# Attention result kept by tokens in a two-layer convolution/attention kernel with a chunked recurrence: transposes moved from ScalarE copies and an early pass to TensorE at the end

## The chip, the cores and the metric

The kernel runs on one core of a Trainium2 chip. A core has five engines with their own instruction streams: TensorE (PE, matrix products; it loads weights, written PEld in the profile, and streams columns through them into PSUM), VectorE (DVE), ScalarE (ACT), GpSimd (POOL) and SyncE (SP, here the issuer of nearly all transfers). SBUF is the working memory of 128 partitions, PSUM the small memory that PE writes and DVE and ACT read. Transfers between SBUF and the external memory (HBM) run on DMA engines.

The metric is the device time of one execution in microseconds; lower is better. All numbers are float32.

## What is computed

The input x has shape (4, 128, 64, 64): 4 batches, 128 channels, N = 4096 positions, which the second layer calls tokens.

```python
def reference(x, wq, wk, wv, wo, Wq, Wk, Wv, W, V, gamma, beta):
    # layer 0: attention over positions, 64-wide q, k, v; no mask
    q, k, v = (einsum('mc,bcn->bmn', w, xf) for w in (wq, wk, wv))
    att = softmax(einsum('bmi,bmj->bij', k, q), axis=2)
    x = x + einsum('cm,bmn->bcn', wo, einsum('bij,bmj->bmi', att, v))
    # layer 1, by tokens: t is (b, n, c)
    t = x.transpose to (b, n, c)
    t = t + causal_attention(layernorm(t), Wq, Wk, Wv)      # scale 128 ** -0.5
    wx = batchnorm(layernorm(t) @ W.T) * gamma + beta       # mean, var over b and n
    y[i] = sigmoid(wx[i] + y[i-1] @ V.T)                    # recurrence over the tokens
    t = t + y
    return t.transpose back to (b, c, h, w)
```

## The kernel before

B = 4 batches, P = 128, N = 4096, BLK = 512 tokens to a block, NB = 8 blocks, TPB = 4 tiles of 128 tokens to a block.

**Attention.** Both layers run over a list of items (pairs of 128 keys for a block of 512 queries). For each item PE computes scores (line 649 in layer 0, 658 in layer 1), ACT the exponential, DVE the sums, and PE the weighted values (709 and 717), two items later. What is to be done after the last item of a block is spread over the next items as a chain of steps. In layer 1 the chain is this; each `yield` gives the number of items to wait:

```python
def transposed(src, dst, name, engine):
    ps = misc(name)                         # one PSUM bank, two of them in turn
    for j in range(TPB):
        nc.tensor.transpose(ps[:, ts(j, P)], src[:, j], ident)
    engine(dst, ps)

def finish1(b, g):
    def first():
        project(1, b, g, agg, den)          # xs[:, b, block] += attention, by tokens
        mem["xh"] = wk.tile([P, TPB, P], F32, tag="xh2", name="xh2")
        normed(b, g, mem["xh"])             # layernorm by tokens
    def second():
        t = xs[:, b, ts(g, BLK)].rearrange("p (j c) -> p j c", c=P)
        xc = wk.tile([P, BLK], F32, tag="xc", name="xc")
        transposed(t, xc, "tT_ps", nc.scalar.copy)
        nc.sync.dma_start(out=x2[b, :, ts(g, BLK)], in_=xc)
        mem["xhT"] = wk.tile([P, BLK], F32, tag="xhT2", name="xhT2")
        transposed(mem["xh"], mem["xhT"], "xh2T_ps", nc.vector.tensor_copy)
    def third():
        wp = misc("wx_ps")
        nc.tensor.matmul(wp, lhsT=wf, rhs=mem["xhT"], start=True, stop=True)
        ...
        nc.vector.bn_stats(stats[:, b * NB + g], wp)
        nc.scalar.copy(                     # wx overwrites the tokens in xs, sorted by step
            xs[:, b, ts(g, BLK)].rearrange("p (s c) -> p s c", c=CPB),
            wp.rearrange("p (c s) -> p s c", s=STEPS))
    yield 1, first
    yield 3, second
    yield 1, third
```

The tokens after attention are needed again at the end, so they are put aside in HBM (`x2`), here turned to channels by tokens.

**Recurrence.** It is cut into NCH = 256 chunks of STEPS = 16 tokens, which run side by side as 256 columns; each chunk is warmed up with the 12 tokens before it. In all 28 rounds of 4 batches, each of a matmul, an addition by DVE and a sigmoid by ACT:

```python
with ... tc.tile_pool(name="ps_y", bufs=2, space=PSUM) as ps_y:
    xr = xrp.tile([P, B, N], F32, name="xr")
    for b in range(B):
        nc.sync.dma_start(out=xr[:, b], in_=x2[b])
    ...
    by_step = xs.rearrange("p b (g s c) -> p b s g c", s=STEPS, c=CPB)
    def step(b, s):
        wx = by_step[:, b, s % STEPS]
        ...                                 # y: where the state goes; for s >= 0 it replaces wx
        ps = grid(ps_y.tile([P, NCH], F32, tag=f"y{b}", name="y_ps"))
        nc.tensor.matmul(ps, lhsT=vf, rhs=prev[b], start=True, stop=True)
        z = grid(yp.tile([P, NCH], F32, tag=f"z{b}", name="z"))
        nc.vector.scalar_tensor_tensor(z, in0=wx, scalar=scale, in1=ps, op0=ALU.mult, op1=ALU.add)
        nc.scalar.activation(y, z, AF.Sigmoid, bias=shift)
```

**Residual.** At the end ACT sorts the states back to token order and DVE adds them to the loaded tokens:

```python
def residual(b):
    for h in range(2):
        for g in range(h * NB // 2, (h + 1) * NB // 2):
            y = yp.tile([P, BLK], F32, tag="yt", name="yt")
            nc.scalar.copy(y.rearrange("p (c s) -> p c s", s=STEPS),
                           xs[:, b, ts(g, BLK)].rearrange("p (s c) -> p c s", c=CPB))
            t = xr[:, b, ts(g, BLK)]
            nc.vector.tensor_tensor(t, t, y, ALU.add)
        half = slice(h * N // 2, (h + 1) * N // 2)
        nc.sync.dma_start(out=out[b, :, half], in_=xr[:, b, half])
```

Beside it stands a test of the warm-up, the gap test: two matmuls and a square for each batch compare the states at chunk borders, and a flag decides whether a slower general path has to run (it does not for this input; it lies in the program all the same).

Of the kernel before, what the change touches and what calls it, by code (L numbers as in the profile page):

```python
# [9 lines left out]
F32 = mybir.dt.float32  # L10
AF = mybir.ActivationFunctionType
ALU = mybir.AluOpType
AX = mybir.AxisListType
PSUM = bass.MemoryType.PSUM

P = 128
BLK = 512
# [6 lines left out]
def general_path(  # L24
# [16 lines left out]
    nc = tc.nc  # L41
    B, C, N = x.shape
# [3 lines left out]
    NB = N // BLK  # L46
    TPB = BLK // P
# [5 lines left out]
    xs = xpool.tile([P, B, N], F32, name="xs")  # L53
# [229 lines left out]
    with tc.tile_pool(name="wx", bufs=1) as wxp, tc.tile_pool(name="fwork", bufs=3) as wk:  # L283
        wx = wxp.tile([P, N, B], F32, name="wx")
        stats = wxp.tile([P, B * NB, nc.vector.BN_STATS_DIM], F32, name="stats")
        with tc.tile_pool(name="ps_ln", bufs=2, space=PSUM) as ps_ln, tc.tile_pool(
            name="ps_wx", bufs=3, space=PSUM
        ) as ps_wx:
            for b in range(B):

                def project(blk, xhat, b=b):
                    wp = ps_wx.tile([P, BLK], F32, tag="w", name="wx_ps")
                    nc.tensor.matmul(wp, lhsT=wf, rhs=xhat, start=True, stop=True)
                    nc.vector.bn_stats(stats[:, b * NB + blk, :], wp)
                    nc.scalar.copy(wx[:, ts(blk, BLK), b], wp)

                layernorm(b, ps_ln, wk, project)


        mv = wxp.tile([P, nc.vector.BN_AGGR_DIM], F32, name="mv")  # L300
        nc.vector.bn_aggr(mv, stats)
        scale = wxp.tile([P, 1], F32, name="scale")
        nc.vector.tensor_scalar(scale, mv[:, 1:2], BN_EPS, None, ALU.add)
        nc.vector.reciprocal(scale, scale)
        nc.scalar.activation(scale, scale, AF.Sqrt)
        nc.vector.tensor_tensor(scale, scale, gamma, ALU.mult)
        shift = wxp.tile([P, 1], F32, name="shift")
        nc.vector.tensor_tensor(shift, mv[:, 0:1], scale, ALU.mult)
        nc.vector.tensor_tensor(shift, beta, shift, ALU.subtract)

        STEPS = BLK // B
        with tc.tile_pool(name="ys", bufs=3) as ysp, tc.tile_pool(name="ps_y", bufs=2, space=PSUM) as ps_y:

            def preload(kb):
                wn = wk.tile([P, STEPS, B], F32, tag="wn", name="wn")
                nc.vector.tensor_scalar(wn, wx[:, ts(kb, STEPS), :], scale, shift, ALU.mult, ALU.add)
                ps = ps_y.tile([P, STEPS, B], F32, tag="y", name="y_ps")
                nc.tensor.matmul(ps, lhsT=ident, rhs=wn, start=True, stop=False, skip_group_check=True)
                return ps

            nblk = N // STEPS
            prev = None
            nxt = preload(0)
            for kb in range(nblk):
                ps = nxt
                y = ysp.tile([P, STEPS, B], F32, tag="y", name="y")
                for t in range(STEPS):
                    if prev is not None:
                        nc.tensor.matmul(
                            ps[:, t, :], lhsT=vf, rhs=prev, start=False, stop=t == STEPS - 1, skip_group_check=True  # L330
                        )
                    nc.scalar.activation(y[:, t, :], ps[:, t, :], AF.Sigmoid)
                    prev = y[:, t, :]
                    if t == STEPS // 2 and kb + 1 < nblk:
                        nxt = preload(kb + 1)
                o = ysp.tile([P, B, STEPS], F32, tag="o", name="o")
                nc.gpsimd.tensor_tensor(o, xs[:, :, ts(kb, STEPS)], y.rearrange("p t b -> p b t"), ALU.add)
                nc.sync.dma_start(out=out[:, :, ts(kb, STEPS)].rearrange("b c n -> c b n"), in_=o)

# [1 line left out]
def fast_path(  # L343
# [39 lines left out]

    xs = xpool.tile([P, B, N], F32, name="xs")

    x2 = dram.tile([B, P, N], F32, name="x2")

    def load(name, shape, *parts):
        t = const.tile(shape, F32, name=name)
# [45 lines left out]
    with tc.tile_pool(name="batch", bufs=1) as batch, tc.tile_pool(name="rows", bufs=2) as rowp, tc.tile_pool(  # L435
# [116 lines left out]
        def transposed(src, dst, name, engine):  # L552

            ps = misc(name)
# [3 lines that stand above are left out]
# [25 lines left out]
        def finish1(b, g):  # L583
            agg, den = bs[b].agg, bs[b].den
            mem = {}

            def first():
                project(1, b, g, agg, den)
                mem["xh"] = wk.tile([P, TPB, P], F32, tag="xh2", name="xh2")
                normed(b, g, mem["xh"])  # L590

            def second():
                t = xs[:, b, ts(g, BLK)].rearrange("p (j c) -> p j c", c=P)
                xc = wk.tile([P, BLK], F32, tag="xc", name="xc")
                transposed(t, xc, "tT_ps", nc.scalar.copy)
                nc.sync.dma_start(out=x2[b, :, ts(g, BLK)], in_=xc)
                mem["xhT"] = wk.tile([P, BLK], F32, tag="xhT2", name="xhT2")
                transposed(mem["xh"], mem["xhT"], "xh2T_ps", nc.vector.tensor_copy)

# [3 lines that stand above are left out]
                if b == B - 1 and g == NB - 1:  # L603
                    in_range()
                nc.vector.bn_stats(stats[:, b * NB + g], wp)  # L605

                nc.scalar.copy(  # L607
                    xs[:, b, ts(g, BLK)].rearrange("p (s c) -> p s c", c=CPB),
                    wp.rearrange("p (c s) -> p s c", s=STEPS),
# [5 lines that stand above are left out]
# [184 lines left out]


    with tc.tile_pool(name="xr", bufs=1) as xrp, tc.tile_pool(name="y", bufs=2) as yp, tc.tile_pool(
        name="ps_y", bufs=2, space=PSUM
    ) as ps_y:
        xr = xrp.tile([P, B, N], F32, name="xr")
        for b in range(B):
            nc.sync.dma_start(out=xr[:, b], in_=x2[b])

        mv = xrp.tile([P, nc.vector.BN_AGGR_DIM], F32, name="mv")
        nc.vector.bn_aggr(mv, stats)
# [11 lines left out]
        nc.gpsimd.memset(start[:, :, 0:1], 0.0)  # L821
        prev = [None] * B
        grid = lambda t: t.rearrange("p (g c) -> p g c", c=CPB)

        def step(b, s):

            wx = by_step[:, b, s % STEPS]
            if s == -1:
                y = grid(start[:, b, 1:])
            elif s < 0:  # L830
                y = grid(yp.tile([P, NCH], F32, tag=f"y{b}", name="y"))
            else:
                y = wx
            if prev[b] is None:
                nc.scalar.activation(y, wx, AF.Sigmoid, scale=scale, bias=shift)
            else:
                ps = grid(ps_y.tile([P, NCH], F32, tag=f"y{b}", name="y_ps"))
                nc.tensor.matmul(ps, lhsT=vf, rhs=prev[b], start=True, stop=True)  # L838
                z = grid(yp.tile([P, NCH], F32, tag=f"z{b}", name="z"))
                nc.vector.scalar_tensor_tensor(z, in0=wx, scalar=scale, in1=ps, op0=ALU.mult, op1=ALU.add)  # L840
                nc.scalar.activation(y, z, AF.Sigmoid, bias=shift)  # L841
            prev[b] = grid(start[:, b, :NCH]) if s == -1 else y

        for s in range(-WARM, STEPS):
            for b in range(B):
# [1 line left out]

        def residual(b):

            for h in range(2):  # L850
                for g in range(h * NB // 2, (h + 1) * NB // 2):
                    y = yp.tile([P, BLK], F32, tag="yt", name="yt")
                    nc.scalar.copy(  # L853
                        y.rearrange("p (c s) -> p c s", s=STEPS),
                        xs[:, b, ts(g, BLK)].rearrange("p (s c) -> p c s", c=CPB),
                    )
                    t = xr[:, b, ts(g, BLK)]
                    nc.vector.tensor_tensor(t, t, y, ALU.add)
                half = slice(h * N // 2, (h + 1) * N // 2)
                nc.sync.dma_start(out=out[b, :, half], in_=xr[:, b, half])  # L860

        for b in range(B - 1):
            residual(b)
# [2 lines left out]
        gap = xrp.tile([P, B], F32, name="gap")  # L866
        for b in range(B):
            ps = ps_y.tile([P, NCH], F32, tag=f"y{b}", name="gap_ps")
            nc.tensor.matmul(grid(ps), lhsT=ident, rhs=by_step[:, b, STEPS - 1], start=True, stop=False)
            nc.tensor.matmul(ps, lhsT=minus, rhs=start[:, b, 1:], start=False, stop=True)  # L870
            sq = yp.tile([P, NCH], F32, tag=f"y{b}", name="sq")
            nc.scalar.activation(sq, ps, AF.Square, accum_out=gap[:, b : b + 1])
# [68 lines left out]
```

## Time and profile before

| What | Value |
|---|---|
| device time, median of 3 | 2187.38 us (2187.21 to 2190.06) |
| span of the profiled execution | 2186.7 us |
| granted PE clock, mean | 0.989 |
| attention stage (to the last attention matmul) | 0 to about 2076 us |
| last block, statistics, loads of xr | 2076 to 2092 us |
| recurrence | 2093 to 2147 us |
| residual and stores | 2145 to 2187 us |
| stores of the result, out_x<-xr | 8 of 1 MB each, landing in 3.8 to 5.6 us |

How to read the profile. A group is named by its line in the kernel, its engine and operation, and by the tiles that it writes and reads (`tT_ps<-ident,xs`). "x128" is a count. PE takes an fp32 matmul as two passes, so 512 columns show as two rows. Busy times of pipelined matmuls overlap: a row's duration includes its latency, and the distance between starts is what it takes from the engine. "Idle before" is the time for which the engine stood still ahead of the group, with what ended it. The page's 40 slices show busy shares in tenths, and PEclk the share of the full PE clock that was granted. The chain is the sequence of work that ended last, followed back from the end. A window row gives the busy time of each engine between two points of time, the granted clock, the busy share of the DMA engines and the GB/s they moved.

### The profile page before, as it was taken

To read this page: it belongs to the slowest core of one execution; us is meant where nothing else is said; L and a number is where in the kernel's file an instruction comes from. 1 tells how busy PE (TensorE), PEld (TensorE's weight loads), DVE (VectorE), ACT (ScalarE), POOL (GpSimd) and SP (SyncE) were. 2 spreads that over 40 slices of the span, in tenths; PEclk is the share of its full clock that TensorE was granted. 3 is DMA by queue.
4 is the path that set the end of the run, shared out by engine and by line. 5 is a ranking of instruction groups with operands and counts; after the bars stand their busy time and mean duration, and the time that the engine had idled before them with its cause. 6 is when DMAs were issued, how large, how long until landed. Compare 5 with 4: busy or idle time off the path is not lost.

```text
span 2186.7 us, 30521 instructions
## 1 busy us (share of the span) xinstructions
PE 2113.2 (97%) x12204; PEld 939.7 (43%) x12204; DVE 1440.6 (66%) x2703; ACT 1057.2 (48%) x1162; POOL 104.5 (5%) x207
## 2 busy tenths in 40 slices
PE   6999999999999999999999999999999999999973
PEld 2333354444333345444333335444433334544452
DVE  3888865444788875544688876445478887544486
ACT  4666633333566643333466653332366664332378
POOL 0000010000000010000000001000000001000000
PEclk9999999999999999999999999999999999999986
DMA  6000011000000001000000001100000000000033
GB/s 222 1 1 1 1 31 47 5 6 5 6 1 1 1 20 39 20 10 5 6 1 1 1 1 39 39 6 5 5 6 1 1 1 6 10 10 6 5 159 155
DMA packets 30134, 48.74 MB, mean 22 GB/s; under 512 B 3104, under 2 KB 20256, under 8 KB 28448
## 3 DMA queue, kind: packets, MB, share of 16 engines
q1 hardware_dynamic: 28096, 46.15, 6.1%
q8 instruction: 98, 1.61, 0.3%
q10 hardware_dynamic: 1888, 0.56, 0.1%
q14 instruction: 52, 0.43, 0.1%
HBM read 25.72 MB, written 16.78 MB: 19 GB/s over the span
## 4 chain that ended last, share of the span: by engine, by line
PE 92%; ACT 4%; DVE 2%; DMA 1%; POOL 0%; issue 0%; ACTq 0%; DVEq 0%
PE s_ps L658 21%; PE acc L717 21%; PE s_ps L649 20%; PE acc L709 19%; PE o_ps L527 2%; ACT yt L853 1%; PE den_ps L521 1%; PE kr_ps L469 1%; PE wx_ps L602 1%; ACT xs L841 1%; PE r_ps L512 1%; PE xhT_ps L556 1%; PE v_ps L481 1%; ACT y L841 1%; DVE dsum L689 1%; PE xh2T_ps L556 1%
## 5 line engine op out<-in xcount | busy, mean ns | idle before, releaser
L689 DVE TENSOR_TENSOR dsum<-dsum,p 128x1024 f32<-128x1024 f32 x676 | 828.0, 1225 | 465.6 <-ACT p L665 336.7
L663 ACT ACTIVATE p<-s_ps,nshift 128x1024 f32<-128x1024 f32 x512 | 571.2, 1116 | 354.8 <-PE s_ps L649 335.3
L665 ACT ACTIVATE p<-s_ps 128x1024 f32<-128x1024 f32 (+2 forms) x288 | 274.2, 952 | 564.0 <-PE s_ps L658 462.5
L709 PE MATMUL acc<-p,v 64*64 64x512 f32 x4096 | 532.3, 590 | 1.7 <-ACT half L728 1.7
L649 PE MATMUL s_ps<-swap,kr 64*64 64x512 f32 x2048 | 528.2, 593 | 0.4 <-ACT p L663 0.4
L649 PE MATMUL s_ps<-kr 64*64 64x512 f32 x2048 | 528.2, 593 | 0.0
L658 PE MATMUL s_ps<-rows,xhT 128*128 128x512 f32 (+3 forms) x1152 | 503.9, 559 | 0.0
L717 PE MATMUL acc<-p,xh 128*128 128x512 f32 (+3 forms) x1152 | 501.5, 557 | 0.0
L717 PEld LDWEIGHTS acc<-p,xh 128*128 128x128 f32 x1152 | 215.6, 190 | 241.3 <-issue 231.8
L658 PEld LDWEIGHTS s_ps<-rows,xhT 128*128 128x128 f32 x1152 | 211.0, 190 | 227.1 <-issue 189.7
L709 PEld LDWEIGHTS acc<-p,v 64*64 64x64 f32 x4096 | 155.1, 133 | 284.6 <-issue 265.6
L649 PEld LDWEIGHTS s_ps<-swap,kr 64*64 64x64 f32 x2048 | 136.9, 133 | 130.9 <-issue 123.9
L649 PEld LDWEIGHTS s_ps<-kr 64*64 64x64 f32 x2048 | 137.0, 133 | 128.3 <-issue 123.7
L429 POOL TENSOR_TENSOR ln_rstd<-ln_var,mhalf 128x4 f32<-128x4 f32 x64 | 66.1, 1033 | 1218.6 <-DVE ln_var L544 1218.6
L697 DVE TENSOR_TENSOR dsum<-dsum,p 128x256 f32<-128x256 f32 (+1 forms) x120 | 56.1, 500 | 72.4 <-POOL p L669 72.4
L687 DVE COPY dsum<-p 128x1024 f32<-128x1024 f32 x60 | 41.4, 690 | 67.3 <-ACT p L665 57.6
L532 DVE SCALAR_TENSOR_TENSOR xs<-o_ps,recs,xs 128x128 f32<-128x128 f32 x256 | 73.0, 345 | 8.9 <-PE o_ps L527 2.8
L548 DVE TENSOR_SCALAR xh<-xs,ln_mv,ln_rstd 128x128 f32<-128x128 f32 x256 | 71.4, 343 | 2.2
L669 POOL TENSOR_SCALAR_AFFINE_SELECT p<-p 128x128 f32<-128x128 f32 x128 | 34.4, 292 | 681.7 <-ACT p L665 681.7
L541 DVE BATCH_NORM_STATS2 ln_st<-xs 128x6 f32<-128x128 f32 x256 | 63.7, 273 | 0.0
L840 DVE SCALAR_TENSOR_TENSOR z<-xs,scale,y_ps 128x256 f32<-128x256 f32 x108 | 48.6, 481 | 5.9 <-PE y_ps L838 5.2
L607 ACT COPY xs<-wx_ps 128x512 f32<-128x512 f32 x32 | 18.7, 584 | 69.6 <-DVE stats L605 69.6
(101 smaller groups left out, 1109.2 us busy)
## 6 DMA issues: line engine op xcount, KB each, us to landing
xs<-in_x SPq DMA_DIRECT2D x16, 512.0 KB, 7.2
xs<-in_xT SPq DMA_DIRECT2D x32, 256.0 KB, 3.2
x<-xc SPq DMA_DIRECT2D x32, 256.0 KB, 2.0
xr<-x SPq DMA_DIRECT2D x4, 2048.0 KB, 11.8
out_x<-xr SPq DMA_DIRECT2D x8, 1024.0 KB, 4.0
swap<-kr SPq DMA_DIRECT2D x32, 128.0 KB, 2.2
wo<-in_c_woT ACTq DMA_DIRECT2D x2, 32.0 KB, 4.3
wqT<-in_a_wqT ACTq DMA_DIRECT2D x1, 64.0 KB, 5.9
```

Of the source, the lines that this page charges most:

```text
L429: nc.gpsimd.tensor_tensor(y, var, mhalf[:, : y.shape[-1]], ALU.pow)
L532: nc.vector.scalar_tensor_tensor(t, in0=op[:, ts(j, P)], scalar=rec[:, j : j + 1], in1=t, op0=ALU.mult, op1=ALU.add)
L541: nc.vector.bn_stats(st[:, j], xs[:, b, ds(g * BLK + j * P, P)])
L548: nc.vector.tensor_scalar(dst[:, j], xs[:, b, ds(g * BLK + j * P, P)], mv[:, j, 0:1], y[:, j : j + 1], ALU.subtract, ALU.mult)
L649: nc.tensor.matmul(ps[c * M : c * M + M, off : off + n], lhsT=bs[it.b].kr[part, h, ds(t % (NT // 2) * P + c * M, M)], rhs=rows[h], start=True,
L658: nc.tensor.matmul(ps[:, off : off + n], lhsT=lhsT, rhs=rhs, start=True, stop=True)
L663: nc.scalar.activation(it.p[:, :off], ps[:, :off], AF.Exp, bias=nshift)
L665: nc.scalar.activation(it.p[:, :off], ps[:, :off], AF.Exp, scale=float(P) ** -0.5)
L689: nc.vector.tensor_tensor(flat, flat, it.p, ALU.add)
L697: nc.vector.tensor_tensor(den[:, h, q0:], den[:, h, q0:], it.p[:, o : o + n], ALU.add)
L709: nc.tensor.matmul(bt.acc[h * M : h * M + M, r], lhsT=bt.v[part, t], rhs=it.p[part, o : o + n], start=it.first, stop=it.last,)
L717: nc.tensor.matmul(bt.acc[:, 0, q0:], lhsT=bt.xh[:, t], rhs=it.p[:, o : o + n], start=it.first and h == 0, stop=it.last and h == 1,)
```

## The change

It keeps layer 1's data by tokens and drops the turn to channels before the store to x2. `first()` stores the tokens as they are, in rows of 128 channels (512 bytes); `second()` only makes the transposed layernorm. The output is then also written by tokens, and the last turn to channels is made on the host when the result is returned.

The states of the recurrence are made by channels, so they must be turned once, at the end: PE transposes each step's 128 chunks into PSUM, and DVE adds them from PSUM to the tokens. ACT's sorting copies go. For this the states are no longer written in place over wx: the first four steps go to a new tile `early`, the others over the wx of steps that have been used, so that 128 chunks of one step lie side by side. The tokens are loaded with the chunk on the partition and 16 steps of 128 channels in a row. PSUM is shared out anew: `ps_y` has one buffer for each batch instead of two, and the transposes get four banks.

```diff
             def first():
                 project(1, b, g, agg, den)
+                nc.sync.dma_start(
+                    out=x2[b, ts(g, BLK)].rearrange("(j p) c -> p j c", p=P),
+                    in_=xs[:, b, ts(g, BLK)].rearrange("p (j c) -> p j c", c=P),
+                )
                 mem["xh"] = wk.tile([P, TPB, P], F32, tag="xh2", name="xh2")
                 normed(b, g, mem["xh"])
 
             def second():
-                t = xs[:, b, ts(g, BLK)].rearrange("p (j c) -> p j c", c=P)
-                xc = wk.tile([P, BLK], F32, tag="xc", name="xc")
-                transposed(t, xc, "tT_ps", nc.scalar.copy)
-                nc.sync.dma_start(out=x2[b, :, ts(g, BLK)], in_=xc)
                 mem["xhT"] = wk.tile([P, BLK], F32, tag="xhT2", name="xhT2")
                 transposed(mem["xh"], mem["xhT"], "xh2T_ps", nc.vector.tensor_copy)
 ... (cut)
-        name="ps_y", bufs=2, space=PSUM
-    ) as ps_y:
-        xr = xrp.tile([P, B, N], F32, name="xr")
+        name="ps_y", bufs=1, space=PSUM
+    ) as ps_y, tc.tile_pool(name="ps_r", bufs=4, space=PSUM) as ps_r:
+        HALVES = NCH // P
+        by_chunk = lambda t: t.rearrange("b (h q s) c -> b h q s c", q=P, s=STEPS)
+        xr = xrp.tile([P, B, HALVES, STEPS, P], F32, name="xr")
         for b in range(B):
-            nc.sync.dma_start(out=xr[:, b], in_=x2[b])
+            for h in range(HALVES):
+                nc.sync.dma_start(out=xr[:, b, h], in_=by_chunk(x2)[b, h])
 ... (cut)
+        pair = lambda t: t.rearrange("p (h q) -> p h q", q=P)
+        early = xrp.tile([P, B, TPB, NCH], F32, name="early")
+        late = xs.rearrange("p b (r h k q) -> p b k r h q", h=HALVES, r=TPB, q=P)
+        def states(b, s):
+            return pair(early[:, b, s]) if s < TPB else late[:, b, s // TPB - 1, s % TPB]
 ... (cut: step() writes its state to states(b, s) for s >= 0)
         def residual(b):
-            for h in range(2):
-                for g in range(h * NB // 2, (h + 1) * NB // 2):
-                    y = yp.tile([P, BLK], F32, tag="yt", name="yt")
-                    nc.scalar.copy(
-                        y.rearrange("p (c s) -> p c s", s=STEPS),
-                        xs[:, b, ts(g, BLK)].rearrange("p (s c) -> p c s", c=CPB),
-                    )
-                    t = xr[:, b, ts(g, BLK)]
-                    nc.vector.tensor_tensor(t, t, y, ALU.add)
-                half = slice(h * N // 2, (h + 1) * N // 2)
-                nc.sync.dma_start(out=out[b, :, half], in_=xr[:, b, half])
+            for h in range(HALVES):
+                for s0 in range(0, STEPS, TPB):
+                    ps = ps_r.tile([P, TPB, P], F32, tag="r", name="yT_ps")
+                    for j in range(TPB):
+                        nc.tensor.transpose(ps[:, j], states(b, s0 + j)[:, h], ident)
+                    t = xr[:, b, h, ds(s0, TPB)]
+                    nc.vector.tensor_tensor(t, t, ps, ALU.add)
+                nc.sync.dma_start(out=by_chunk(out)[b, h], in_=xr[:, b, h])
 ... (cut: the same change of layout in the general path, which does not run here)
-    return np.asarray(r.results[0]["out_x"]).reshape(b, c, h, w)
+    y = np.asarray(r.results[0]["out_x"])
+    return np.ascontiguousarray(y.transpose(0, 2, 1)).reshape(b, c, h, w)
```

More of the change, by code (lines that the diff above doesn't have):

```diff
@@ L311, in general_path @@
         STEPS = BLK // B
-        with tc.tile_pool(name="ys", bufs=3) as ysp, tc.tile_pool(name="ps_y", bufs=2, space=PSUM) as ps_y:
+        with tc.tile_pool(name="ys", bufs=3) as ysp, tc.tile_pool(
+            name="ps_y", bufs=2, space=PSUM
+        ) as ps_y, tc.tile_pool(name="ps_o", bufs=2, space=PSUM) as ps_o:
             def preload(kb):
@@ L337, in general_path @@
                 nc.gpsimd.tensor_tensor(o, xs[:, :, ts(kb, STEPS)], y.rearrange("p t b -> p b t"), ALU.add)
-                nc.sync.dma_start(out=out[:, :, ts(kb, STEPS)].rearrange("b c n -> c b n"), in_=o)
+                op = ps_o.tile([P, B, P], F32, tag="o", name="oT_ps")
+                for b in range(B):
+                    nc.tensor.transpose(op[:, b, :], o[:, b, :], ident)
+                oT = ysp.tile([P, B, P], F32, tag="oT", name="oT")
+                nc.vector.tensor_copy(oT, op)
+                nc.sync.dma_start(out=out[:, ts(kb, STEPS), :].rearrange("b n c -> n b c"), in_=oT)
 @with_exitstack
@@ L384, in fast_path @@
     xs = xpool.tile([P, B, N], F32, name="xs")
-    x2 = dram.tile([B, P, N], F32, name="x2")
+    x2 = dram.tile([B, N, P], F32, name="x2")
     def load(name, shape, *parts):
@@ L823, in fast_path @@
         grid = lambda t: t.rearrange("p (g c) -> p g c", c=CPB)
+        pair = lambda t: t.rearrange("p (h q) -> p h q", q=P)
+        assert HALVES * TPB == NB
+        early = xrp.tile([P, B, TPB, NCH], F32, name="early")
+        late = xs.rearrange("p b (r h k q) -> p b k r h q", h=HALVES, r=TPB, q=P)
+        def states(b, s):
+            return pair(early[:, b, s]) if s < TPB else late[:, b, s // TPB - 1, s % TPB]
         def step(b, s):
@@ L828, in step @@
             if s == -1:
-                y = grid(start[:, b, 1:])
+                y = start[:, b, 1:]
             elif s < 0:
-                y = grid(yp.tile([P, NCH], F32, tag=f"y{b}", name="y"))
+                y = yp.tile([P, NCH], F32, tag=f"y{b}", name="y")
             else:
-                y = wx
+                y = states(b, s)
             if prev[b] is None:
-                nc.scalar.activation(y, wx, AF.Sigmoid, scale=scale, bias=shift)
+                nc.scalar.activation(grid(y), wx, AF.Sigmoid, scale=scale, bias=shift)
             else:
[L837 to L842, printed above, removed]
+                ps = ps_y.tile([P, NCH], F32, tag=f"y{b}", name="y_ps")
+                nc.tensor.matmul(ps if s < 1 else pair(ps), lhsT=vf, rhs=prev[b], start=True, stop=True)
+                z = yp.tile([P, NCH], F32, tag=f"z{b}", name="z")
+                nc.vector.scalar_tensor_tensor(
+                    grid(z), in0=wx, scalar=scale, in1=grid(ps), op0=ALU.mult, op1=ALU.add
+                )
+                nc.scalar.activation(y, z if s < 0 else pair(z), AF.Sigmoid, bias=shift)
+            prev[b] = start[:, b, :NCH] if s == -1 else y
         for s in range(-WARM, STEPS):
@@ L868, in fast_path @@
             ps = ps_y.tile([P, NCH], F32, tag=f"y{b}", name="gap_ps")
-            nc.tensor.matmul(grid(ps), lhsT=ident, rhs=by_step[:, b, STEPS - 1], start=True, stop=False)
+            nc.tensor.matmul(pair(ps), lhsT=ident, rhs=prev[b], start=True, stop=False)
             nc.tensor.matmul(ps, lhsT=minus, rhs=start[:, b, 1:], start=False, stop=True)
@@ L928 @@
     }
-    y = nc.dram_tensor("out_x", (b, c, h * w), F32, kind="ExternalOutput").ap()
+    y = nc.dram_tensor("out_x", (b, h * w, c), F32, kind="ExternalOutput").ap()
     layer0 = [ins[n] for n in ("in_x", "in_c_wqT", "in_c_wkT", "in_c_wvT", "in_c_woT")]
```

## The prediction

> **What bounds the kernel now.** I read the page from the top: busy shares, then the 40 slices, then the chain that ended last.
>
> ```profile
> PE 2113.2 (97%) x12204; PEld 939.7 (43%) x12204; DVE 1440.6 (66%) x2703; ACT 1057.2 (48%) x1162; POOL 104.5 (5%) x207
> ...
> PE   6999999999999999999999999999999999999973
> ...
> ACT  4666633333566643333466653332366664332378
> ...
> PE 92%; ACT 4%; DVE 2%; DMA 1%; POOL 0%; issue 0%; ACTq 0%; DVEq 0%
> ```
>
> TensorE (PE) is full in every slice but the first and the last two, and 92% of the chain is PE. So the span has two parts: the attention stage, up to about 2076 us, where only PE instructions count, and a tail of 111 us, where PE falls to 7 and 3 tenths. In the attention stage ScalarE (ACT) and VectorE (DVE) are half idle and work taken from them is worth nothing. The timeline of PE shows how tightly it is packed:
>
> ```profile
> 316.83 0.60 PE L556 MATMUL tT_ps<-ident,xs 128*128 128x128 f32 x4
> 317.27 0.60 PE L556 MATMUL xh2T_ps<-ident,xh 128*128 128x128 f32 x4
> 317.70 1.88 PE L658 MATMUL s_ps<-rows,xhT 128*128 128x512 f32 x4
> ```
>
> Starts are 0.44 us apart although each row lasts 0.60: matmuls overlap, so what a group of four transposes takes from PE is the distance to the next start, 0.44 us. No row has an idle time, so every such group delays all that follows.
>
> The tail is read in windows (the first columns are window, length, then busy time of PE, PEld, DVE, ACT, POOL, and the granted clock):
>
> ```profile
> 2092.00:2145.00 53.00, 51.56 (x216) 34.88 (x216) 47.80 (x107) 50.83 (x111) 0.00 (x0) 0.93 0.13 54
> 2145.00:2187.00 42.00, 4.10 (x20) 2.95 (x18) 23.27 (x37) 34.04 (x44) 0.00 (x0) 0.60 0.50 202
> ```
>
> The first is the recurrence, in which PE, DVE and ACT turn together. The second is the residual stage: PE does almost nothing, and ACT is busy from 2145.4 to 2179.1. The groups by form give the price of its parts (busy and mean ns | idle before):
>
> ```profile
> L853 ACT COPY yt<-xs 128x512 f32<-128x512 f32 x32 | 31.8, 1074 | 0.0
> ...
> L838 PE MATMUL y_ps<-xs,vf 128*128 128x256 f32 x120 | 27.4, 390 | 0.0
> ...
> L858 DVE TENSOR_TENSOR xr<-xr,yt 128x512 f32<-128x512 f32 x32 | 22.2, 692 | 11.5 <-ACT yt L853 11.5
> ...
> L556 PE MATMUL tT_ps<-ident,xs 128*128 128x128 f32 x128 | 20.0, 277 | 0.4 <-DVE xs L532 0.4
> ```
>
> ACT's copies follow each other without idle time; DVE's adds wait 11.5 us for them. So the stage is ACT's reordering copy, 32 times. The last line's 20.0 us is busy time with overlaps, not what leaves the chain.
>
> **What the Trainium skill says.** "TensorE: Matmul & The Clock Gate", Part 1: the PE clock halves after an idle window of about 3.4 us. The trace agrees: the last regular matmul of the residual stage ends at 2148.9, and the clock falls within 2152 to 2154:
>
> ```profile
> 2152.00:2154.00 2.00, 0.00 (x0) 0.00 (x0) 1.08 (x3) 2.00 (x3) 0.00 (x0) 0.93 0.95 393
> 2154.00:2156.00 2.00, 0.00 (x0) 0.00 (x0) 1.26 (x2) 2.00 (x4) 0.00 (x0) 0.50 0.32 131
> ```
>
> The same page, Part 4, says that a transpose by PE took about 275 ns in one kernel (here 272 to 273 ns at full clock, 462 to 473 ns for the last block's at clock 0.50), and that transposes do not count as PE activity for the clock as matmuls do. No stretch of this trace has transposes alone, so the second point is open here; it is the largest doubt below. "VectorE: DVE Perf Modes", The perf-mode tier table: an add of two fp32 tensors runs at one element a cycle from SBUF or PSUM alike. The trace agrees as far as it goes: the fp32 add grows from 692 ns at 512 elements to 1225 at 1024, 1.04 ns an element, and the PSUM-fed z of the recurrence takes 481 ns for 256. "DMA: Bandwidth & Descriptors", Specifications: pieces of 512 B and more run at line rate; here 256 KB of token rows (512 B pieces) loads in 3.2 us.
>
> **Part 1, attention stage.** Removed: four PE transposes and an ACT copy in each of 32 blocks. 31 of them lie in the packed stream at 0.44 us (0.436 from 317.27 to 317.70 and 316.83 to 317.27): 31 x 0.436 = **13.5 us off the chain**. The last block's group (2078.43) falls where PE waits for DVE's layernorm: 0. The 32 ACT copies (585 ns, 18.7 us) are hidden: 0. Moved: the store to x2 now reads xs itself, before wx overwrites it four items later. An item of layer 1 takes 3.43 us of PE (eight 512-column passes of 0.429), an item of layer 0 half of that, so the store has 7 to 14 us; stores landed in 2.0 us so far, and the 512 B form should land in about the 3.2 of the token loads. In the program order of the DMA queue some stores stand behind transfers that wait up to 11.3 us for PE, so one or two could come close. I count 0.
>
> **Part 2, recurrence.** Same number of steps, same columns. A step takes 0.453 us (four in 1.81) on all three engines; PE needs 2 x 0.214 = 0.429 of it. The reordering into 2 x 128 columns changes no count. The instruction order of the changed kernel shows 7 single transposes put among the last 60 matmuls, each 0.107 us (0.43/4) against a slack of 0.024 a step: I charge **+0.4 us**. One PSUM buffer per batch instead of two should cost nothing, since a batch's next matmul needs the state that was made from the old buffer anyway.
>
> **Part 3, residual stage.** Removed: ACT's 32 copies, which set the pace of 0.98 us a block (32 copies and the four squares: 2145.4 to 2179.1). Added: 128 PE transposes, 32 groups of four at 0.43 us when warm; and the adds now read PSUM. Their price: 692 ns from SBUF plus some 50 for PSUM (a 128-column operation costs 345 from PSUM against 278 from SBUF), less an overlap of 0.06 to 0.09 (the four 345-ns updates fill 1.12 us, 0.26 each): 0.66 to 0.72, I take 0.69. 32 x 0.69 = 22.1 us, plus 0.4 for the small operations of the flag. The last z ends at 2145.8; with +0.4 the adds run from 2146.2 to 2168.7, if DVE is the bound. Before, the last add ended at 2179.76 and the span 6.94 us later (last store and end). Stores come every 2.8 us, 1 MB each, 380 GB/s; the window above shows 393 GB/s at 95% busy, so they just keep up; I add 0.3. End at 2168.7 + 6.94 + 0.3 = 2175.9 on the old time axis: **10.8 us off**, the 0.4 of part 2 included.
>
> Sum with a warm PE: 2187.4 - 13.5 - 10.8 = **2163.1 us**.
>
> **Rivals.** (a) PE goes cold in the residual stage and becomes its bound. For it: after 2146 PE does transposes almost only, and part 4 above. Against it: a transpose stream at DVE's pace still occupies 0.43/0.69 = 62% of PE, and 8 matmuls of the gap test (16 passes of 0.214) are spread among them. Price: about 5 us after the end of the recurrence the clock would halve with some 11.6 us (at full clock) of PE work left of 16.4 (121 transposes of 0.107 and 16 passes of 0.214; until then DVE can take 7 groups and PE be 4 buffers ahead, 4.8 us), which then takes 23.2: from 2151.2 to 2174.4, and the last add ends near 2175.5 instead of 2168.7. That is 7 us lost, total **2170**. I hold it nearly as likely as not. (b) The stores bind. For it: 380 GB/s asked, about 400 possible. Against it: the first store is issued after only 4 adds and each MB needs 2.6 us. If the rate were 350, the end would move by 2 to 3 us: 2166. (c) A new wait in the attention stage: ACT's copy of wx must now wait until the x2 store has read xs. If it held up ACT's in-order queue, and so the exponentials, by 1 us in a third of the blocks, 10 us of the gain would be gone: 2173. The margin of 7 us or more speaks against it. (d) Nothing is gained in the attention stage, because the transposes sat in a gap: the packed starts above speak against it.
>
> **Range and chances.** Warm gives 2163, cold 2170; with nearly equal weights and a little for the other rivals I set **2165.5 us**, 80% range **2160 to 2172**. Faster by over 2% would need 43.7 us, more than the parts touched can give: 0.02. Slower by over 2% needs a stall of 68 us beyond the gain: 0.01. Within 2%: 0.97.
>
> **What would show it.** Part 1: PE's last attention matmul (acc) ends at about 2063 instead of 2076, with no tT row, and ACT's wx copy shows no wait for a transfer. Part 2: steps still 1.81 us for four. Part 3: the last add ends 22 to 23 us after the last z, the adds wait little for PE, and the clock column stays at 1.00 after the recurrence. If it reads 0.50 there, with adds waiting for PE and transposes of 460 ns, rival (a) holds. A landing time of the stores far above 4 us means (b). The prediction fails if the last add ends later than 2165 in the new trace, or if the attention stage shrinks by less than 12 us.

## The result and the profile after

The changed kernel takes **2163.28 us** (median of 4 runs, 2162.26 to 2164.89); beside it the kernel before takes 2188.36 (4 runs, 2187.21 to 2190.06). The ratio is **0.9885, 95% interval 0.9868 to 0.9903**: about 1.15% faster. The turn of the output to channels, which the host now makes, lies outside this time. The profiled executions give 2186.7 and 2161.9 us, a difference of 24.8 us, and all that follows is an account of these 24.8. In the attention stage a line of the changed kernel has a number 7 higher than before (L563 was L556), in the recurrence and the residual stage 20 to 23 higher (L879 was L858).

The page of the changed kernel, busy shares and two rows of its 40 slices:

```profile
PE 2115.7 (98%) x12204; PEld 941.5 (44%) x12204; DVE 1435.2 (66%) x2703; ACT 1007.9 (47%) x1098; POOL 104.5 (5%) x207
...
PE   7999999999999999999999999999999999999978
...
PEclk9999999999999999999999999999999999999989
```

PE has as many instructions as before (128 transposes taken away in layer 1, 128 added at the end), but its last two slices now stand at 7 and 8 tenths, where they stood at 7 and 3. ACT has lost 64 instructions, 49 us.

The same part as the two windows shown of before, recurrence and then residual stage (window, length, busy time of PE, PEld, DVE, ACT, POOL, granted clock, DMA share, GB/s):

```profile
2081.00:2134.00 53.00, 53.00 (x230) 37.96 (x230) 48.62 (x109) 50.24 (x111) 0.00 (x0) 0.95 0.29 123
2134.00:2162.00 28.00, 17.61 (x134) 15.00 (x132) 19.26 (x35) 2.40 (x9) 0.00 (x0) 0.87 0.74 303
```

From the last z of the recurrence (written by DVE in each step) to the end it is now 27.9 us instead of 40.9, and DVE, no longer ACT, works through it. The groups by form between 2132 and 2162 us (count, busy us, mean ns, idle before) answer to the rows of the copy and the add (28 more transposes, which read `early`, have a row of their own):

```profile
L879 DVE TENSOR_TENSOR xr<-xr,yT_ps 128x512 f32<-128x512 f32 x32 | 19.4, 682 | 0.0
L877 PE MATMUL yT_ps<-ident,xs 128*128 128x128 f32 x93 | 12.8, 275 | 0.0
```

The adds stand without idle time, where they had waited 11.5 us for ACT. The 32 of them fill 19.4 us, so their starts are 0.60 us apart although one lasts 682 ns. Read in finer windows:

```profile
2136.00:2140.00 4.00, 4.00 (x33) 3.70 (x32) 4.00 (x8) 0.78 (x4) 0.00 (x0) 1.00 0.72 295
2140.00:2144.00 4.00, 4.00 (x34) 3.80 (x33) 4.00 (x7) 0.48 (x2) 0.00 (x0) 1.00 1.02 426
2144.00:2148.00 4.00, 4.00 (x33) 3.36 (x32) 4.00 (x8) 0.47 (x2) 0.00 (x0) 1.00 1.02 422
2148.00:2152.00 4.00, 3.60 (x26) 2.40 (x24) 4.00 (x11) 0.00 (x0) 0.00 (x0) 1.00 1.01 414
2152.00:2156.00 4.00, 0.00 (x0) 0.00 (x0) 1.26 (x3) 0.00 (x0) 0.00 (x0) 0.87 1.00 406
```

Three things are to be seen. The clock stays at 1.00 for as long as PE transposes. DVE is full until its last add. And from 2140 to 2156 the DMA engines are full at 406 to 426 GB/s, also after DVE has finished: the stores have become the last limit, and the span ends 8.6 us after the last add, where it was 6.9. The stores also pile up: their time from issue to landing grows from 3.9 us for the first to 6.5 for the last (min, median and max of the eight):

```profile
DMA to landing us min/median/max: 3.9/4.4/6.5
```

From the timelines of PE and DVE, the difference by parts (minus is a gain):

| part | predicted | measured |
|---|---|---|
| first score matmul to the end of the last block's attention | -13.5 us | -12.8 (its start came 0.2 later) |
| from there to the first matmul of the recurrence | 0 | -0.15 |
| first matmul of the recurrence to its last z | +0.4 | +0.9 |
| last z to last add (33.9 before) | -11.5 | -14.6 |
| last add to end (6.94 before) | +0.3 | +1.7 |
| sum | -24.3 | -24.8 |

The total came out within 0.5 us in the profile, but out of terms that are off by up to 3 us and cancel. The experiments take them one by one.

### The profile page after: what moved, and what is told of

Its sections match the earlier page's. It is cut to its first block, busy times and chain, and to the rows that moved or that the text cites. A ratio compares the mean times of both kernels' runs of the same rounds, so it can differ in the third digit from the quotient of the medians.

```text
span 2161.9 us, 30424 instructions
## 1 busy us (share of the span) xinstructions
PE 2115.7 (98%) x12204; PEld 941.5 (44%) x12204; DVE 1435.2 (66%) x2703; ACT 1007.9 (47%) x1098; POOL 104.5 (5%) x207
```

## Experiments

The theory: PE's time for the transposes of layer 1 came off the span, and at the end DVE's adds from PSUM, on a warm PE, took the place of ACT's copies. The rivals of the prediction are tested with it. Every kernel is the changed one with the edit shown; ratios are to the kernel before. It took 2188.34 us (median) beside the first four experiments (turn put back, copy, gap test, later turn) and 2189.95 beside the other four, so across these two groups the ratios are the better comparison.

### The turn put back: does its PE time make the span?

The transposes and the copy come back into layer 1; nobody reads their result, and everything else stays by tokens.

```diff
             def second():
+                t = xs[:, b, ts(g, BLK)].rearrange("p (j c) -> p j c", c=P)
+                xc = wk.tile([P, BLK], F32, tag="xc", name="xc")
+                transposed(t, xc, "tT_ps", nc.scalar.copy)
```

> The changed kernel with the removed turn put back in every block of layer 1: four PE transposes of the tokens and ACT's copy of them, which nobody then reads; the store still takes the tokens from xs. So only the residual part of the change is left. Theory (the turn's PE time was on the path, except where PE waited for the layernorm): the attention stage grows by what it shrank, 12.6 us, so about 2176; in three of the 31 blocks, those in which layer 0 of the next batch has begun, the growth is 0.1 us instead of 0.44. Rival (the gain of the attention stage came from ACT's queue or from the PSUM banks): growth differs block by block from 0.44. Rival (all the gain is in the residual stage): no growth, 2163.

Measured: 2176.82 us (2175.39 to 2178.32), ratio 0.9948 (0.9931 to 0.9965), 13.5 us above the changed kernel in the medians. In the profile the attention stage, from its first score matmul on, grew by 12.8 us, to 2043.80, and the kernel before has 2043.76. From the last z on the two kernels agree within 0.2 us. (The span of the profile grew by 11.8 only, because the clock rose earlier in the recurrence, see below.) So the turn accounts for the whole difference of the attention stage; the next experiment parts its transposes from its copy.

Block by block, though, the growth isn't even. It is 0.43 to 0.45 us in the packed blocks, as predicted, but 0.06 in two blocks: the last layer-1 blocks of the first two batches, whose turn falls among layer-0 items of the next batch. The timeline of PE shows why. First the kernel before, at the end of its second batch:

```profile
1067.22 1.04 PE L709 MATMUL acc<-p,v 64*64 64x512 f32 x8
1068.19 0.66 PE L556 MATMUL tT_ps<-ident,xs 128*128 128x128 f32 x4
1069.74 1.09 PE L556 MATMUL xh2T_ps<-ident,xh 128*128 128x128 f32 x4 [0.90 <-DVE xh L548]
```

Then the changed kernel at the same place:

```profile
1061.24 1.04 PE L716 MATMUL acc<-p,v 64*64 64x512 f32 x8
1063.76 1.10 PE L563 MATMUL xh2T_ps<-ident,xh 128*128 128x128 f32 x4 [1.48 <-DVE xh L555]
```

The brackets give the idle time before the row and what ended it. PE waits there for DVE's layernorm in both kernels, because a layer-0 item is over in 1.7 us. With the turn gone, from the start of the acc row to that of xh2T still takes 2.52 us: the wait grew from 0.90 to 1.48. Here the turn had sat in a gap.

At the third border the change even lost 0.66 us. The wait is 1.48 there too, but the clock column fell (the two borders side by side):

```profile
1055.00:1072.00 17.00, 14.67 (x122) 5.74 (x118) 13.05 (x32) 7.27 (x8) 1.01 (x1) 1.00 0.05 16
1568.00:1585.00 17.00, 15.52 (x114) 5.90 (x114) 12.56 (x31) 6.54 (x8) 1.01 (x1) 0.90 0.05 16
```

and in the timeline of the second stretch one group of matmuls runs almost twice as long as the 1.04 it takes elsewhere:

```profile
1578.51 1.95 PE L716 MATMUL acc<-p,v 64*64 64x512 f32 x8
```

One block of the fourth batch gave 1.52 us instead of 0.44: in it xh2T had also waited 0.9 us for DVE's copy of the next rows. That wait is absent from the changed kernel and comes back with the turn; the list of PE's waits in this experiment (total us, times, longest) has it beside the layernorm's (whose longest, 3.7, is that of the very last block):

```profile
PE xh2T_ps L563 <- DVE xh L555: 6.3, 4, 3.7
...
PE xh2T_ps L563 <- DVE rows L521: 0.9, 1, 0.9
```

The tile tT_ps takes its buffers from the same pool as r_ps, of which the rows are copied; that the pool is the cause was not tried by itself. Added up: 27 x 0.437 + 1.52 + 0.06 + 0.07 - 0.66 = 12.8 us. Without the fall of the clock it would have been some 13.5, the predicted figure, but by other parts than 31 equal ones.

### Only the copy put back: is ACT hidden?

```diff
             def second():
+                xc = wk.tile([P, BLK], F32, tag="xc", name="xc")
+                nc.scalar.copy(xc, xs[:, b, ts(g, BLK)])
```

> The changed kernel with only ACT's part of the removed turn put back: a copy of 128x512 (585 ns or a little more, from SBUF) in every block of layer 1, no transposes. Theory: ACT is half idle in the attention stage, so the copy is hidden: 2163, attention stage unchanged within 0.5 us. Rival (ACT's in-order queue holds up the exponentials): up to 32 x 0.6 = 19 us more, 2175 to 2182.

Measured: 2162.83 us (2161.08 to 2164.35), ratio 0.9881 (0.9865 to 0.9898), the time of the changed kernel. In the profile the blocks moved by 0.01 us or less, apart from two places: at the third border no fall of the clock occurred, and 0.7 us were regained; and at the very start of layer 0, before any of these copies, the clock fell to half for 3.4 us, which cost 1.0. ACT's 32 copies cost nothing. At the three borders, though, this is not because ACT is idle. There the copy holds up the exponential behind it, and with it PE's next matmuls by 0.47 us; the list of PE's waits has it three times:

```profile
PE s_ps L658 <- ACT p L672: 0.7, 3, 0.2
```

The wait for the layernorm takes this up: it is 1.00 us instead of 1.48. The rival is true at these three places, and is paid for by a wait that was there anyway.

### Without the gap test: does a PE with transposes alone go cold?

This kernel leaves out the test that compares the recurrence with its overlap (8 fp32 matmuls and 4 squares); the flag then always says that all is well. From the last z on, PE has only transposes, apart from one matmul of a single column for the flag.

```diff
-        for b in range(B):
-            ps = ps_y.tile([P, NCH], F32, tag=f"y{b}", name="gap_ps")
-            ... (two matmuls and a square with accumulation)
+        nc.gpsimd.memset(gap, 0.0)
```

> The changed kernel without the gap test: its eight matmuls and four squares are left out and the sums that it would give are set to zero, so the flag says that all is well. After the recurrence PE then has transposes only. Theory 1 (transposes count as activity for the PE clock): clock stays at 1.00 until PE is done, transposes last 273 ns, the adds end as before, 19.4 us after the last z; total within 1 us of 2163. Theory 2 (transposes do not count, and the gap test's matmuls kept the clock up): clock 0.50 from about 5 us after the recurrence, transposes of 460 ns, a group every 0.85 us, the last add 4 to 6 us later, total 2167 to 2169.

Measured: 2163.55 us (2162.05 to 2166.05), ratio 0.9889 (0.9872 to 0.9905), again the time of the changed kernel. The windows of this run, after its last z at 2132.4:

```profile
2134.00:2138.00 4.00, 4.00 (x29) 2.75 (x28) 4.00 (x8) 0.00 (x0) 0.00 (x0) 1.00 0.65 266
2138.00:2142.00 4.00, 4.00 (x28) 2.75 (x27) 4.00 (x8) 0.00 (x0) 0.00 (x0) 1.00 1.00 418
2142.00:2146.00 4.00, 4.00 (x29) 2.92 (x28) 4.00 (x7) 0.00 (x0) 0.00 (x0) 1.00 1.00 412
2146.00:2150.00 4.00, 3.89 (x27) 2.52 (x25) 4.00 (x9) 0.00 (x0) 0.00 (x0) 1.00 1.01 416
```

and its view of the transposes' tile (min, median and max ns, first and last start; 32 more read `early`):

```profile
L877 PE MATMUL yT_ps<-ident,xs x96: 272/273/331, 2121.0 to 2149.6; 128*128 128x128 f32 x96
```

For 16 us PE does nothing but transposes, and the clock stays at 1.00, with the 272 to 273 ns of a warm PE. Rival (a) falls for good: it wasn't the gap test that kept PE warm. What is shown is that transposes hold a clock that is up; whether they alone would raise one that has fallen, no run shows.

### The layernorm's transposes of the last block made later

The changed kernel has a wait for the layernorm at the batch borders. This kernel gives the layernorm more time there: its transposes of a batch's last block come two items later, the wx matmul one more (the later turn, below).

```diff
-            yield 3, second
-            yield 1, third
+            more = 2 if g == NB - 1 and b + 1 < B else 0
+            yield 3 + more, second
+            yield 1 + more // 2, third
```

> The changed kernel, but for the last block of batches 0 to 2, whose steps fall among layer 0's half as long items, the transposes of the layernorm come two items later and the wx matmul one more item after them. Theory (PE waited 1.48 us there for the layernorm and 0.86 us for its copy, three times, and once the wait cost clock as well): both waits go, attention stage 3 x 2.3 = 7 us shorter plus 0.7 for the clock, total about 2156. Rival (the wait is only moved to another place, or the DVE queue falls behind): under 2 us, 2161 to 2163.

Measured: **2154.85 us** (2154.56 to 2158.47), ratio 0.9851 (0.9834 to 0.9867), the fastest of all, 8.4 us under the changed kernel in the medians. The three borders became 2.27, 2.27 and 3.00 us shorter, 7.5 together, which is all of the gain in the attention stage. At the first border, in the timeline of PE:

```profile
552.87 0.66 PE L563 MATMUL xh2T_ps<-ident,xh 128*128 128x128 f32 x4
...
557.47 1.12 PE L609 MATMUL wx_ps<-xhT,wf 128*128 128x512 f32 x2 [0.35 <-DVE xhT L564]
```

The wait for the layernorm is gone, and 0.35 of some 0.9 us of the second wait, for the copy of xhT, is left. The remaining 0.9 us or so of the 8.4 don't come from these borders; they lie within the spread of the runs, and the stretch from the attention stage to the first row `start` varies by 1.4 us among kernels that do the same in it (see below).

### Smaller stores

Since the stores end last, they could begin earlier: after every add instead of every four, 32 stores of 256 KB in pieces of 2 KB instead of 8 of 1 MB in pieces of 8 KB.

```diff
                     nc.vector.tensor_tensor(t, t, ps, ALU.add)
-                nc.sync.dma_start(out=by_chunk(out)[b, h], in_=xr[:, b, h])
+                    nc.sync.dma_start(out=by_chunk(out)[b, h][:, ds(s0, TPB)], in_=t)
```

> The changed kernel, but each group of four steps is stored as soon as it is added: 32 stores of 256 KB in pieces of 2 KB instead of 8 of 1 MB in pieces of 8 KB. In the changed kernel the DMA engines are 100% busy from 2140 to 2156 and the span ends 8.6 us after the last add, against 6.9 before. Theory (the stores bind the end of the residual stage): the first store starts 1.8 us earlier and the end moves by about that: 2161.5. Rival (the adds bind): the add times are unchanged and only the last store is shorter, 0.75 MB less behind the last add, at 415 GB/s 1.8 us too, but then the DMA engines show gaps between stores. Rival (pieces of 2 KB or the more frequent issue are slower): DMA rate under 400 GB/s, end later than 2163.

Measured: 2164.79 us (2164.61 to 2164.91), ratio 0.9886 (0.9871 to 0.9901): no gain. The first store is issued at 2134.3 instead of 2136.4, and the last add ends at 2153.0, but the end comes 9.9 us after it. The windows show one reason:

```profile
2140.00:2144.00 4.00, 4.00 (x33) 3.70 (x32) 4.00 (x8) 0.47 (x2) 0.00 (x0) 1.00 1.02 384
2144.00:2148.00 4.00, 4.00 (x33) 3.32 (x31) 4.00 (x9) 0.47 (x2) 0.00 (x0) 1.00 1.01 382
2148.00:2152.00 4.00, 3.29 (x23) 2.22 (x22) 4.00 (x10) 0.00 (x0) 0.00 (x0) 1.00 1.02 380
```

As full as before, the DMA moves 380 to 384 GB/s instead of 414 to 426. For 8.39 MB that is 22.0 us against 20.0: the head start of 2 us is spent. A second reason lies behind the last add: SP issues the last of the 32 stores 3.7 us after its add (the changed kernel 0.03 us after), and from 2152 to 2160 the DMA engines are 0.86 and 0.75 busy only. Whether the pieces, the size of a store or their number slows them was not parted. With the same adds and a first store 2.1 us earlier the end came no earlier: the stores, and not the adds, set it.

### Both together

```diff
the edits of the two experiments above
```

> The later transposes of the layernorm at the three batch borders and the small stores together, in the hope of the fastest version. If the two are independent: 2154.9 less 1.8, about 2153. Rival: small stores gain nothing, 2155.

Measured: 2156.73 us (2155.42 to 2159.67), ratio 0.985 (0.9836 to 0.9863), against 0.9851. No better than the later turn alone; the small stores give nothing here either.

### No transpose before the recurrence has ended

The changed kernel's PE does 7 transposes among the last steps of the recurrence. Here the identity they use is made from the last state (times 0, plus the identity), so none can begin earlier.

```diff
+        ident2 = xrp.tile([P, P], F32, name="ident2")
+        nc.vector.scalar_tensor_tensor(ident2, in0=states(B - 1, STEPS - 1)[:, 0],
+                                       scalar=0.0, in1=ident, op0=ALU.mult, op1=ALU.add)
...
-                        nc.tensor.transpose(ps[:, j], states(b, s0 + j)[:, h], ident)
+                        nc.tensor.transpose(ps[:, j], states(b, s0 + j)[:, h], ident2)
```

> The changed kernel with all transposes of states held back until the recurrence is over: they use a copy of the identity matrix that is made from the last state (times zero), by one DVE operation of 128 columns. Theory (each of the 7 transposes among the recurrence's matmuls delays it by 0.09 to 0.1 us, the 0.8 us by which it is longer than before): the recurrence takes 52.4 us from the first matmul to the last z as before the change, instead of 53.2. The first add then waits for the copy and the first four transposes, about 1 us after the last z, so the whole is unchanged within 1 us. Rival (the new layout of states or the single PSUM buffer makes the steps slower): the recurrence stays at 53.2.

Measured: 2163.97 us, one run. From the row `start` (the sigmoid of the last warm-up step, whose states each batch keeps for the gap test) to the last z it takes 30.37 us, as the kernel before (30.38); the changed kernel takes 31.05. So neither the new layout nor the single PSUM buffer costs anything: the 0.67 us are the 7 transposes, 0.096 each. They can be seen in the changed kernel's timeline of PE:

```profile
2118.51 4.23 PE L859 MATMUL y_ps<-xs,vf 128*128 128x256 f32 x18
2122.57 0.27 PE L877 MATMUL yT_ps<-ident,xs 128*128 128x128 f32 x1
2122.68 4.22 PE L859 MATMUL y_ps<-xs,vf 128*128 128x256 f32 x18
```

Nine steps and one transpose take 4.17 us from start to start, where nine steps alone take 9 x 0.453 = 4.08. What the wait for the new identity costs is in the timeline of DVE in this experiment:

```profile
2133.14 0.29 DVE L872 SCALAR_TENSOR_TENSOR ident<-xs,ident 128x128 f32<-128x128 f32 x1 [0.57 <-ACT xs L864]
2134.31 14.44 DVE L884 TENSOR_TENSOR xr<-xr,yT_ps 128x512 f32<-128x512 f32 x24 [0.88 <-PE yT_ps L882]
```

The first add comes 1.74 us after the last z instead of at once: more than was saved is spent again.

### The turn put back into the kernel with the later turn

If the border blocks gave nothing only because PE waited there, then with the wait gone the turn should cost 0.44 us there as well.

```diff
the edit of the later turn, and the three lines of the first experiment
```

> The kernel with the later transposes of the layernorm (2154.9), with the removed turn put back in every block, PE transposes and ACT's copy. Theory (the turn cost 0.44 us in every packed block, and only the wait for the layernorm hid it at the batch borders): now it costs 0.44 in all 31, the attention stage is 13.5 to 14.5 us longer, about 2168.9. Rival (at the batch borders the turn fills other slack): 12.4 us, 2167.3, with 0.1 in three blocks.

Measured: 2169.54 us (2167.67 to 2169.93), ratio 0.9908 (0.9893 to 0.9923). Against the later turn alone that is 12.5 us more by the ratios (14.7 in the medians, which belong to the two groups), and the attention stage of the profile grew by 13.3. That is near what 31 blocks of 0.44 give, but not by that path: at the borders the growth was 0.01 or less, because the 0.35 us for which PE had still waited for xhT are gone, so the turn filled that gap instead; and the block with 0.9 us of waiting for the rows was back. So 27 blocks of 0.44, one of 1.5 and three of nothing make the 13.3. At the borders the rival holds, and the theory's sum was nearly met only through the one block that neither of the two counted.

## Why the prediction was right, and where its terms were not

The prediction set 2165.5 us between a warm case of 2163.1 and a cold one of 2170. The warm case came true, 2163.28.

**Attention stage.** The mechanism and the price were right: 0.43 to 0.45 us in the packed blocks, shown by putting the turn back. The step that failed is the count, "31 of them lie in the packed stream". The timeline had been read in the middle of a batch; three blocks at the batch borders lie where PE waits for the layernorm, and gave 0.06, 0.07 and -0.66. One block gave 1.1 us more than its transposes. In sum that made 12.8 instead of 13.5. Of the rivals, (d), the transposes sat in a gap, holds for three blocks in 31. (c), a wait of ACT's copy of wx for the new store, didn't happen: in ACT's waits the copy waits for DVE's statistics, and for no transfer:

```profile
ACT xs L614 <- DVE stats L612: 73.1, 28, 11.3
```

The stores in rows of 512 bytes landed in 2.3 us (median; 4.1 at most), inside the 7 to 14 that were allowed.

**Recurrence.** The charge of 0.4 us was for 7 transposes at 0.107 less what slack there is; they took 0.67. The slack of 0.024 a step was no slack: nine steps and a transpose take almost the sum of both. The other 0.2 us lie in the first steps: the clock rose 6.0 us after the first matmul of the recurrence, against 5.7 in the kernel before. From the end of the attention stage to the first `start` row it took 39.5 us in the kernels before and after, but 38.1 in the kernels with the turn put back and with the later turn, which do the same there. The difference is the moment at which the clock rises: over the ten traces it lies 2.9 to 6.0 us after the first matmul, and the row `start` follows it, 20.7 to 22.2 us after that matmul. So 1.4 us of any such comparison of profiles can be luck. In these traces the clock moves in steps: ahead of this rise it is low for 13.7 us in three of them and for 17.1 in seven, 3.4 us apart, and each fall at a border lasts 3.4 us. What sets the moment at which a step begins was not tried.

**Adds.** This was the largest miss. 692 ns and 50 for PSUM, less an overlap, made 0.69; the row shows 682 ns busy and 0.60 from start to start. PSUM as a source added nothing to the duration. The surcharge of 50 came from two operations that differ in more than their source: the 345 ns are those of a multiply and add with two tensors and a scalar, and the layernorm's own 128-column operation takes 343 in the same trace though it reads SBUF alone:

```profile
L548 DVE TENSOR_SCALAR xh<-xs,ln_mv,ln_rstd 128x128 f32<-128x128 f32 x256 | 71.4, 343 | 2.2
```

The overlap of 0.08 was as estimated. (With the prediction's own terms, 692 + 50 less 60 to 90, the range is 0.65 to 0.68, not 0.66 to 0.72.) 32 x 0.09 is 2.9 of the 3.1 us by which the stage beat its estimate, and the flag's three small operations, which cost 0.2 together instead of 0.4, make the rest.

**Stores.** They were predicted to just keep up at 380 GB/s asked, with 0.3 us for it. But adds 0.60 apart finish 1 MB every 2.4 us, 437 GB/s, more than the 406 to 426 that the DMA gave. So rival (b) holds in a mild form: a better rate than it feared, and yet the last limit. It took back 1.4 us of the 3.1.

**Clock.** Rival (a), held "nearly as likely as not", rested on the Trainium skill, "TensorE: Matmul & The Clock Gate", Part 4, that transposes do not count as PE activity. In this kernel they do, as far as holding the clock goes: 16 us of transposes alone at clock 1.00. The measurement decides, and the weight given to the cold case, which moved the prediction 2.4 us off, was not needed.

## What to carry to other kernels

What removing work from a full engine brings is its start-to-start distance in the packed stretches, and nothing where that engine waits for another: list the waits by place before multiplying by the count, and look at the borders between phases, for a wait found there (here 7.5 us at three borders) can be worth more than half of what the removal brought (12.8). When a stage is sped up, work out the rate at which it then feeds the stores, since a limit that "just keeps up" at the old rate becomes the end of the kernel at the new one. A sum that comes out right is no proof of its terms; compare them part by part.

## What the hardware showed that was not expected

- Transposes by PE in fp32, 272 to 273 ns each, held the granted clock at 1.00 for 16 us with no other PE work.
- A wait of PE of 1.48 us at a batch border was followed by a fall of the clock in 4 of 12 cases, once in each of the four kernels that have it, at the first or the third border (a group of 1.95 instead of 1.04 us, 0.7 us lost); waits of 0.9 to 1.0 us at the borders were not, in nine cases. The Trainium skill, "TensorE: Matmul & The Clock Gate", Part 1, speaks of an idle window of about 3.4 us; here less than half of it was enough at times.
- Adds of two fp32 tensors, one of them in PSUM, 512 columns: 0.60 us apart when back to back.
- Stores of 256 KB with pieces of 2 KB moved 380 to 384 GB/s, stores of 1 MB with pieces of 8 KB 406 to 426, the DMA engines being full in both.
- The low stretches of the PE clock came in steps: 3.4, 13.7 and 17.1 us, that is 1, 4 and 5 times 3.4.
